# A two-layer gated cross-attention kernel: the place of the q_r products among the transposes

## The chip, the core and the metric

The kernel runs on one core of one Trainium2 chip. Its engines have queues of their own: TensorE (PE, matrix products and transposes), VectorE (DVE), ScalarE (ACT), GpSimd (POOL) and SyncE (SP, which here only issues DMAs). The metric is device time in microseconds, and lower is better.

## The reference

`x` has four batch rows of 512 tokens with 512 features; `ctx_512` is a context of 4 x 512 x 128. Two layers follow each other, each a gated mixing with the context and a gated feed-forward part:

```python
x = x + tanh(g_xattn[0]) * L0_xattn(ctx_512, layernorm(x), ...)   # top-k adjacency, 4 x 512 x 512
x = x + tanh(g_ffn[0])   * L0_ffn(layernorm(x), ...)              # Hadamard, 8-bit activations, ternary weights
x = x + tanh(g_xattn[1]) * L1_xattn(layernorm(x), ctx_512, ...)   # 16 heads, below
x = x + tanh(g_ffn[1])   * L1_ffn(layernorm(x), ...)              # 8-bit activations, ternary weights
```

The change lies in the third line. Cut to what matters, that attention is:

```python
q_hk  = (hidden_q @ Wq.T)                                 # 16 heads of 128
q_big = einsum('bshk,hkq->bshq', q_hk, w_kc_q)            # 384 per head
q_big = q_big * cos_q + rotate_half(q_big) * sin_q
kv_r  = kv_c * cos_k + rotate_half(kv_c) * sin_k
q_r   = einsum('bshq,hqr->bhsr', q_big, W_qr)             # 64 per head
k_r   = einsum('bld,hdr->bhlr', kv_r, W_kr)
attn  = softmax(einsum('bhsr,bhlr->bhsl', q_r, k_r))
ctx_c = einsum('bhsl,bld->bhsd', attn, kv_r)
out   = (ctx_c through w_kc_kv and Wo, summed over the heads)
```

## The kernel before

The attention of the second layer is the spine of the program. `attention` (L860) walks over 32 pairs of heads, eight for each batch row, in four steps `j` for the four token tiles of 128. A pair is an object of class `Pair` (L737). While the scores of the current pair `cur` are worked on, the queries of the next pair `nxt` are made:

- `scores(j)` (L798): the scores of both heads for token tile j into PSUM (`pss`, L806 and L809), their negated row maximum on VectorE (`nm`, L814), the exponential with its sum on ScalarE (`pp`, L817), and the scaling by 1/sum on ScalarE (L820).
- `head(i)` (L744): the query of one head of the next pair (`pqh`, L747), copied to `qh` by ScalarE.
- `rope(i)` (L755): two products with `wc` (`pb`, L762), then on VectorE a product with the cosine (`ro`, L770) and one or two with the sine (`rs`, L772 or L775), and on GpSimd their sum, back into `ro` (L776). `rope(2)`, called in step 3, makes the last two of the six `ro` tiles.
- `turn(j)` (L823): for each head four transposes of the probabilities of token tile j into one PSUM tile (`ppt`, L828), and ScalarE's copy to `pT` (L829). These PSUM tiles come from the pool `pst`, which has two.
- `rotated()` (L779): the load of the next `kr` (L783), then q_r of both heads of the next pair in one PSUM tile (`pr`): three steps, each of one product for the upper half of the partitions (L733) and one for the lower (L735), over the six `ro` tiles. The last step needs the two tiles of `rope(2)`. ScalarE copies `pr` to `qr` (L793).
- `attended()` (L831): eight products of `pT` with the context (`pc`, L836), copied to `cxo` by ScalarE (L841). `added()` (L844): eight products with the folded output weights (`po`, L848), and on VectorE the addition to x (L853).

`pr`, `pss`, `pqh`, `pb`, `pc` and `po` share the four PSUM tiles of the pool `ps`; `kr`, `qr` and `wr` have one buffer each, `ro` has seven, `pT` two.

Behind the spine runs background work, drawn step by step from generators at the `yield` of each j: for batch rows 1 to 3 first the adjacency of the first layer (20 rounds of top-k on VectorE, `m` L436 and `work` L441, given a low priority with `high_priority(offset=-FILL)`), then its feed-forward part (`feed0`); while the last batch row is in the attention, the weights of the last feed-forward part and that part itself (`feed1`) for the earlier rows. Row 0 goes through the first layer before the attention starts, and row 3 through the last feed-forward part after it ended.

The order on each engine isn't the order of the text. A scheduler in the compiler goes through the instructions with priorities that follow the text, and takes an instruction of lower priority when, by its own estimate, the one ahead of it isn't ready. The text's order is thus a preference; each engine's resulting queue is fixed when the program is built.

Of the kernel before, what the change touches and what calls it, by code (L numbers as in the profile page):

```python
# [17 lines left out]
NT = S // P  # L18
# [15 lines left out]
def flamingo_kernel(  # L34
# [661 lines left out]
    def hidden_T(b):  # L696
        mv, r = ln_stats([xs[b, j] for j in range(NT)], f"q{b}")
        t = hp.tile([P, NC, S], F32, tag="hT", name=f"hT_{b}", bufs=1)
        for j in range(NT):
            n = wp.tile([P, D], F32, tag="pp", name=f"nq_{b}_{j}", bufs=7)  # L700
            ln_tile(n, xs[b, j], j, mv, r)
            pt = tr_ps(f"phT_{b}_{j}")
            for c in range(NC):
                nc.tensor.transpose(pt[:, c, :], n[:, c * P : (c + 1) * P], ident)
            nc.scalar.copy(t[:, :, j * P : (j + 1) * P], pt)
        hT[b] = t
# [15 lines left out]
    def out_weights(b, g):  # L722

        oms = []
        for h in (2 * g, 2 * g + 1):
            om = hp.tile([P, D], F32, tag="om", name=f"om_{b}_{h}")
            nc.sync.dma_start(om, om_d[h])
            oms.append(om)
        return oms
# [125 lines left out]
    def begin(b, g):  # L855
        p = Pair(b, g)
        p.wqs, p.wc, p.wr = query_weights(b, g)
        return p

    def attention(first):  # L860


        order = [(b, g) for b in range(B) for g in range(NG)]
        cur = first
        for at, (b, g) in enumerate(order):
            nxt = begin(*order[at + 1]) if at + 1 < len(order) else None
            cur.oms = out_weights(b, g)
            fresh = nxt is not None and nxt.b != b
            for j in range(NT):
                cur.scores(j)  # L870
                if nxt:
                    if j == 0:
                        if fresh:
                            hidden_T(nxt.b)
                        nxt.head(0)
                    elif j == 1:
                        nxt.rope(0)
                        nxt.head(1)
                    elif j == 2:
                        nxt.rope(1)  # L880
                    else:
                        nxt.rope(2)
                if j > 1:
                    cur.turn(j - 2)
                yield b, g
            if nxt:
                nxt.rotated()
            cur.turn(NT - 2)
            cur.turn(NT - 1)
            cur.attended()  # L890
            cur.added()
            if g == NG - 1 and b < B - 1:
                for j in range(NT):
                    d = dram.tile([P, D], F32, tag=f"xd{b}_{j}", name=f"xd_{b}_{j}")
                    nc.sync.dma_start(d, xs[b, j])
                    spilled[b, j] = d
            cur = nxt
# [67 lines left out]
    for _ in attention(first):  # L965
        done += 1
        while job < len(jobs):
            gen, cost, until = jobs[job]
            start = jobs[job - 1][2] if job else 0
            want = cost * (done - start) / (until - start)  # L970
            ended = False
            while spent < want or done >= until:
                if f"g{B - 2}" in reached:

                    break
                try:
                    spent += next(gen)
                except StopIteration:
                    ended = True
                    break  # L980
            if not ended:
                break
            if done < until:

                jobs[job] = (iter(()), 0.0, until)
                break
            job, spent = job + 1, 0.0
# [127 lines left out]
```

## Time and profile before

| | |
|---|---|
| median of 3 runs | 2082.72 us (2080.54 to 2085.15) |
| the profiled execution | 2086.76 us, of which the profile's span is 2085.0 us |
| TensorE clock granted, mean | 0.972 of full |
| up to 285 us: first layer of row 0 and the preparation | TensorE busy 172.2 of 285 us |
| 285 to 1930 us: the attention with its background | TensorE busy 1556.2 of 1645 us |
| 1930 to 2085 us: the last pair and the last feed-forward | TensorE busy 135.8 of 155 us |
| q_r products (L733 and L735) | 192 matrix passes each, median 592 ns, the two halves side by side |
| transposes (L828) | 1024 passes, 272 to 475 ns each, overlapping one another |
| rotary addition (L776) | 192 on GpSimd, 1271 ns at the median |
| copies of pT (L829), of qr (L793) | 256 and 32 on ScalarE, 590 and 587 ns |

An instruction group of the profile gives the line, the engine, the operation, output and inputs by their names in the program, the count and the mean length. Lengths of matrix passes overlap, so a run of them is best read from one start to the next. "Idle before" is the time in which the engine stood still just ahead of an instruction, and the arrow names what ended it. In a table of windows each row has the stretch, its length, then busy time and count for TensorE, weight loads, VectorE, ScalarE and GpSimd, the granted clock, the DMA share and GB/s.

### The profile page before, as it was taken

The numbers are of one execution on the slowest core, as the hardware profiler recorded it, in microseconds if no ns is written. First come the engines' busy times: TensorE is split into PE (matmuls) and PEld (weight loads), VectorE is DVE, ScalarE is ACT, GpSimd is POOL, SyncE is SP. The second block draws the span as 40 slices with busy tenths as digits, with TensorE's granted clock in tenths as the row PEclk, the third lists the DMA queues.
The fourth block names the chain that finished last, engine by engine and source line by source line (L and its number), as shares of the span: only waits on it lengthen the run. The fifth ranks groups of instructions, "written<-read, shape, count | busy, mean of one in ns | idle before, by whom it ended". The sixth has DMA issues, their size and how long they took to land.

```text
span 2085.0 us, 21677 instructions
## 1 busy us (share of the span) xinstructions
PE 1864.1 (89%) x7274; PEld 876.8 (42%) x7274; DVE 1589.9 (76%) x3233; ACT 1182.9 (57%) x1982; POOL 331.0 (16%) x316
## 2 busy tenths in 40 slices
PE   1269889999999999999989999999889999999898
PEld 0135433444544444444544444445443444444444
DVE  6997689996675999967668999676645745856775
ACT  6936634354744554455455553554799565567554
POOL 3011121122101121131011211310111200111000
PEclk9779989999999999999999999999999999999999
DMA  7442211110100211111002111110656111111000
GB/s 268 149 141 107 83 37 48 44 46 27 38 20 27 86 50 41 47 32 33 25 27 87 49 47 38 37 33 20 224 185 225 55 31 46 57 32 46 11 16 26
DMA packets 62175, 137.66 MB, mean 66 GB/s; under 512 B 7152, under 2 KB 14704, under 8 KB 58992
## 3 DMA queue, kind: packets, MB, share of 16 engines
q1 hardware_dynamic: 56592, 120.35, 18.2%
q0 software_dynamic: 4320, 14.16, 1.8%
q10 hardware_dynamic: 1152, 1.77, 0.2%
q8 instruction: 58, 0.95, 0.2%
q14 instruction: 53, 0.43, 0.1%
HBM read 116.33 MB, written 19.92 MB: 65 GB/s over the span
## 4 chain that ended last, share of the span: by engine, by line
PE 52%; DVE 29%; ACT 11%; DMA 3%; POOL 2%; issue 2%; ACTq 0%; SPq 0%; POOLq 0%; DVEq 0%
PE pc L836 8%; PE po L848 6%; PE pqh L747 6%; DVE work L441 4%; DVE m L436 4%; DVE nm L814 4%; PE pb L762 3%; PE pzh_f L550 3%; PE pr L733 3%; PE pss L806 3%; PE pu_f L291 2%; DVE rs L775 2%; PE pg_f L291 2%; DVE ro L770 2%; PE pu_g L291 2%; PE pd_g L386 2%
## 5 line engine op out<-in xcount | busy, mean ns | idle before, releaser
L776 POOL TENSOR_TENSOR ro<-ro,rs 128x512 f32<-128x512 f32 x192 | 250.3, 1306 | 1333.8 <-DVE rs L772 722.5
L817 ACT ACTIVATE pp<-pss,nm 128x512 f32<-128x512 f32 x256 | 175.1, 688 | 224.6 <-DVE nm L814 223.9
L747 PE MATMUL pqh<-hT,wq 128*128 128x512 f32 x512 | 240.6, 609 | 4.0 <-ACT pp L817 2.5
L836 PE MATMUL pc<-pT,kv 128*128 128x512 f32 x512 | 233.5, 598 | 6.0 <-ACT pT L829 6.0
L848 PE MATMUL po<-om,cxo 128*128 128x512 f32 x512 | 231.4, 596 | 0.5 <-ACT cxo L841 0.5
L814 DVE TENSOR_REDUCE nm<-pss 128x1 f32<-128x512 f32 x256 | 167.6, 680 | 70.4 <-PE pss L809 70.0
L762 PE MATMUL pb<-qh,wc 128*128 128x512 f32 x384 | 191.7, 617 | 7.4 <-DVE ro L770 3.8
L436 DVE MAX8 m<-work 128x8 f32<-128x512 f32 x304 | 197.6, 680 | 0.5
L441 DVE MATCH_REPLACE8 work<-m,work 128x512 f32<-128x512 f32 x288 | 192.9, 675 | 0.1
L820 ACT ACTIVATE pp<-pp,rsm 128x512 f32<-128x512 f32 x256 | 179.2, 725 | 17.7 <-DVE rsm L819 17.1
L829 ACT COPY pT<-ppt 128x512 f32<-128x512 f32 x256 | 143.2, 590 | 36.9 <-PE ppt L828 36.8
L828 PE MATMUL ppt<-ident,pp 128*128 128x128 f32 x1024 | 149.3, 280 | 11.4 <-ACT pT L829 9.2
L853 DVE SCALAR_TENSOR_TENSOR x<-po,gt,x 128x512 f32<-128x512 f32 x128 | 94.5, 743 | 82.6 <-PE po L848 81.5
L828 PEld LDWEIGHTS ppt<-ident,pp 128*128 128x128 f32 x1024 | 116.4, 142 | 92.5 <-issue 45.6
L806 PE MATMUL pss<-kr,qr 64*128 64x512 f32 x256 | 145.6, 649 | 9.0 <-ACT pp L817 7.5
L747 PEld LDWEIGHTS pqh<-hT,wq 128*128 128x128 f32 x512 | 93.7, 193 | 126.9 <-issue 93.1
L809 PE MATMUL pss<-kr,qr 64*128 64x512 f32 x256 | 145.5, 649 | 0.0
L848 PEld LDWEIGHTS po<-om,cxo 128*128 128x128 f32 x512 | 94.4, 190 | 113.7 <-issue 95.7
L770 DVE TENSOR_TENSOR ro<-pb,cos_q 128x512 f32<-128x512 f32 x192 | 130.4, 679 | 15.1 <-PE pb L762 14.3
L836 PEld LDWEIGHTS pc<-pT,kv 128*128 128x128 f32 x512 | 93.0, 191 | 102.8 <-issue 90.5
L733 PE MATMUL pr<-ro,wr 128*64 128x512 f32 x192 | 100.6, 625 | 29.5 <-POOL ro L776 28.3
L841 ACT COPY cxo<-pc 128x512 f32<-128x512 f32 x64 | 37.5, 586 | 135.3 <-PE pc L836 135.1
(266 smaller groups left out, 3132.8 us busy)
## 6 DMA issues: line engine op xcount, KB each, us to landing
wq<-in_wqh SPq DMA_DIRECT2D x64, 256.0 KB, 2.7
om<-omd SPq DMA_DIRECT2D x64, 256.0 KB, 2.7
wc<-in_wkcq SPq DMA_DIRECT2D x32, 384.0 KB, 3.1
krd<-krs POOLq DMA_DIRECT2D x32, 256.0 KB, 2.5
kr<-krd SPq DMA_DIRECT2D x32, 256.0 KB, 2.7
sa_w1v<-in_gvT SPq DMA_DIRECT2D x8, 1024.0 KB, 5.6
sb_w1v<-in_gvT SPq DMA_DIRECT2D x8, 1024.0 KB, 5.5
wr<-in_wqr SPq DMA_DIRECT2D x32, 192.0 KB, 2.4
```

The source lines that it names most:

```text
L436: nc.vector.max(m8[j], cur[j])
L441: nc.vector.match_replace(works[j], m8[j], cur[j], GONE)
L747: nc.tensor.matmul(pq, self.wqs[i][:, c, :], hT[self.b][:, c, :], start=(c == 0), stop=(c == NC - 1),)
L762: nc.tensor.matmul(pb, self.wc[:, at : at + P], self.qhs[i if i < 2 else o], start=True, stop=True)
L776: nc.gpsimd.tensor_tensor(ro, ro, rs, ALU.add)
L806: nc.tensor.matmul(*args, start=True, stop=True)
L814: nc.vector.tensor_reduce(nm, pss[i], AX.X, ALU.max, negate=True)
L817: nc.scalar.activation(pp, pss[i], AF.Exp, bias=nm, accum_out=sm)
L820: nc.scalar.activation(pp, pp, AF.Copy, scale=rs)
L828: nc.tensor.transpose(pt[:, l, :], pp[:, l * P : (l + 1) * P], ident)
L836: nc.tensor.matmul(pc, kv[self.b][:, l, :], self.pT[i][:, l, :], start=(l == 0), stop=(l == NT - 1),)
L848: nc.tensor.matmul(po, self.cxo[i][:, j * P : (j + 1) * P], self.oms[i], start=(i == 0), stop=(i == 1),)
```

## The change

In `attention`, behind the four steps of a pair, three calls change places: both remaining `turn` calls of the current pair (token tiles 2 and 3) come first in the text, and `rotated()` of the next pair follows them, still ahead of `attended()`.

```diff
                 if j > 1:
                     cur.turn(j - 2)
                 yield b, g
+            cur.turn(NT - 2)
+            cur.turn(NT - 1)
             if nxt:
                 nxt.rotated()
-            cur.turn(NT - 2)
-            cur.turn(NT - 1)
             cur.attended()
             cur.added()
```

Nothing else is edited. The first pair's `rotated()`, called ahead of the attention, and the last pair, which has no next, stay as they are. The priorities of the moved instructions change, and with them the queues that the scheduler builds on TensorE, VectorE and ScalarE, also for background work around them.

## The prediction

> **What bounds the kernel now.** I read the page first, then busy time by window, then who waits for whom on TensorE, then the timeline of single ends of a pair of heads (below: a tail; the tails are numbered 1 to 31, tail n ending where the products with the context of the n-th pair start).
>
> ```profile
> PE 1864.1 (89%) x7274; PEld 876.8 (42%) x7274; DVE 1589.9 (76%) x3233; ACT 1182.9 (57%) x1982; POOL 331.0 (16%) x316
> PE   1269889999999999999989999999889999999898
> ```
>
> The page's first two parts: TensorE is busy 89% of the span, and after the first eighth there are few gaps. So only gaps of TensorE are to be had, and the longest kind that repeats is the one that the change touches:
>
> ```profile
> PE pr L733 <- POOL ro L776: 28.3, 25, 2.9
> PE ppt L828 <- ACT pT L829: 9.2, 29, 1.6
> PE pc L836 <- ACT pT L829: 6.0, 16, 1.9
> ```
>
> The waits of TensorE (total us, times, longest): the products that make q_r (pr) wait for GpSimd's last rotary addition, the transposes (ppt) for ScalarE to empty their PSUM banks, the products with the context (pc) for the last of these copies. 43.5 us together; this is the ceiling. One tail, on TensorE and on ScalarE (start, length, what, and in brackets idle time and releaser):
>
> ```profile
> 354.67 0.59 PE L733 MATMUL pr<-ro,wr 128*64 128x512 f32 x1
> ...
> 355.20 1.09 PE L828 MATMUL ppt<-ident,pp 128*128 128x128 f32 x8
> 356.53 0.44 PE L828 MATMUL ppt<-ident,pp 128*128 128x128 f32 x2 [0.24 <-ACT pT L829]
> 358.05 0.64 PE L733 MATMUL pr<-ro,wr 128*64 128x512 f32 x1 [1.08 <-POOL ro L776]
> ...
> 359.06 0.87 PE L828 MATMUL ppt<-ident,pp 128*128 128x128 f32 x6
> 360.32 0.70 PE L836 MATMUL pc<-pT,kv 128*128 128x512 f32 x1 [0.39 <-ACT pT L829]
> ```
>
> ```profile
> 359.20 0.59 ACT L793 COPY qr<-pr 128x512 f32<-128x512 f32 x1 [2.23 <-PE pr L735]
> 359.68 1.08 ACT L829 COPY pT<-ppt 128x512 f32<-128x512 f32 x2
> ```
>
> The scheduler has already pulled ten of the sixteen transposes in front of the last products of q_r. Six are still behind them, and the copies of these are behind the copy of q_r on ScalarE, which sits 2.23 us waiting. Then the windows from pc to pc (TensorE, weights, VectorE, ScalarE, GpSimd), two with top-k work and two later ones:
>
> ```profile
> 319.40:360.30 40.90, 38.56 (x120) 16.39 (x120) 40.49 (x89) 17.90 (x38) 7.62 (x6) 1.00 0.16 47
> 743.20:784.00 40.80, 38.93 (x122) 16.48 (x120) 40.58 (x90) 18.27 (x39) 7.64 (x6) 1.00 0.17 47
> 1546.10:1588.40 42.30, 38.71 (x124) 16.57 (x123) 19.60 (x40) 39.97 (x54) 7.63 (x6) 1.00 0.78 275
> 1672.00:1742.70 70.70, 69.00 (x284) 30.81 (x283) 43.81 (x71) 44.80 (x69) 7.59 (x6) 1.00 0.12 35
> ```
>
> In the first two VectorE is busy 40.5 of 40.9 us: there the pair lasts as long as VectorE's queue, whatever TensorE does. In the third ScalarE binds (40.0 of 42.3), in the fourth TensorE (69.0 of 70.7). So a gap of TensorE is worth its length in some tails only.
>
> **What the skill says.** The Trainium skill, "TensorE: Matmul & The Clock Gate" (row "Engine queue depth" of the table at the top): weight loads can be pulled ahead, ScalarE's, VectorE's and GpSimd's queues are strictly first in, first out; and its Part 3, "What overlaps and what doesn't", says that matmuls start and end in program order. The trace agrees: the transposes of 359.06 sat behind the waiting product of 358.05, and two copies behind the waiting copy of q_r. So what stands behind what decides here. "Perfetto Trace Analysis", "Identifying Performance Opportunities", warns that matmul busy time overstates how near TensorE is to its best; I use starts and gaps, not busy sums. "GPSIMD Engine Reference", "Key points": GpSimd shares its SBUF interface with VectorE; the rotary addition takes 1.27 us at the median and 2.24 at most, so the arrival of the last operand isn't sharp.
>
> **The change, part by part.** No instruction and no DMA is added or removed. On SyncE the load of kr keeps its place among the others, so it and the loads behind it cost nothing: kr is needed by the next scores, behind eight products pc and eight po (6.9 us each in the chain). On TensorE the orders of both programs, set side by side, show what moves. Before, a tail mostly goes: eight transposes, two steps of q_r, twelve transposes or so, last step of q_r, the rest, pc. After: one step, four transposes, one step, eight, last step, four or none, pc.
>
> (a) Transposes moved in front of the last step. Their arrival of operands is fixed by VectorE and GpSimd, so each fills part of the wait. Counting those behind the last step, before minus after, over the 20 tails that show the wait and keep their surroundings: 66. A transpose is 1.04 us / 8 = 0.13 us. 66 x 0.13 = 8.6 us of the 28.3.
> (b) Copies of the transposes now stand in front of the copy of q_r on ScalarE, so pc doesn't wait: of the 6.0 us, 3.0 in the tails of (d), about 2 in the others.
> (c) The wait of a transpose for its bank (0.24 us each) goes where no wait for q_r follows, as a step of q_r now stands in the gap: six tails, 0.24 us and the 0.19 us ahead of pc, 0.43 us each.
> (Cost) Two steps in a row took 353.33 to 355.20, 1.87 us; one alone 358.05 to 359.06, 1.01. So each split costs 2 x 1.01 - 1.87 = 0.15 us. Ahead of a wait it is hidden; I count five where it isn't: 0.75 us. Without that cover all 26 splits would cost 3.9 us.
>
> (d) VectorE-bound tails (1 to 4, 9 to 12, 17 to 20): 42 of the 66 transposes, 5.5 us, and 3.0 us of (b), 8.5 us at TensorE. But VectorE's idle time over the eleven windows is 8.6 us in all (0.4, 1.8, 0.4; 0.4, 0.2, 1.9, 0.5 twice), and its queue holds the same work. What it can give: bits of that idle time, and top-k steps that the new order puts off to the next stretch (at most three of 0.7 us in the first batch row, one in the others). Bounds 0 and 8.5; I take 3.0.
> (e) The other tails: 24 transposes 3.1 us; six times 0.43 = 2.6; tail 23, where pc waits 1.86 us behind ScalarE's weight work and one step of q_r (1.01) now stands in that gap, 1.0; tail 7, 0.5. 7.2 - 0.75 = 6.4 us.
>
> (d) and (e) make 9.4 us. TensorE has 89 us of idle time between 285 and 1930 us (span minus busy in those windows), 41 of it in these waits; the other 48 are waits for VectorE, ScalarE and POOL that grow when TensorE comes sooner and their producers don't. I take two thirds, 6 us. For the profiled execution, 2086.76 us (span 2085.0, 1.8 around it), this gives 2080.8; that execution lies 4.0 above the median of the runs, 2082.72, so the forecast is 2076.7.
>
> Unknown: in the second batch row the queued feed-forward work near 480 to 570 us is reshuffled (about 6 us of VectorE's work comes one pair sooner, and four GpSimd steps of 0.74 us stand ahead of the last rotary additions in one tail). From its rows it could cost 3 us (4 x 0.74) or gain as much, since TensorE idles 4.2 us in the window from 441.7 to 493.2; I take 0 and keep 3 both ways.
>
> **Rivals.**
> 1. Hidden anyway: VectorE and ScalarE bind more than I allow, (d) gives 0 and half of (e) is taken by the next wait: -3 us, 2079.7; with the reshuffle at a loss, 2082. For it: 98 to 99% in the windows above. Against: VectorE is idle a third of the time in the windows of (e).
> 2. More: all of (d) comes, as VectorE's last 0.5 us per pair wait for po: -6.4 - 8.5 + 3 for later waits, about -12, 2070.8. For it: a wait of 0.47 us of VectorE for po at 369.30. Against: nothing leaves VectorE's queue.
> 3. Slower, through VectorE's queue: the new program puts the updates of x (L853) one top-k step (0.68 us) sooner in the VectorE-bound stretches, 24 of them. If TensorE isn't that much sooner there, VectorE waits for po with the top-k steps and the next row maxima (nm, L814) queued behind, and exponentials and TensorE wait for these. 18 of 24 x 0.68 = 12.2 us, minus 6.4: +6, 2088.6. It decides from some 16 such stalls. For it: x started 0.04 to 0.8 us after po ended in these tails, so there is no slack. Against: TensorE is to come 0.5 to 0.9 us sooner in the same tails, and a step pushed behind a wait doesn't lengthen the queue.
>
> **How the numbers follow.** Forecast 48%, rival 1 25%, rival 2 7%, rival 3 20%. About 0.2%, 4.2 us, is what a measurement of this kernel can tell from no change: faster is below 2078.5, slower above 2086.9. The forecast's own range is 2073 to 2080; part of it (a tenth of the whole) is within 0.2%, and rival 1 lies almost wholly there; a little of rival 3 ends there too. Faster 0.47, same 0.33, slower 0.20. The range reaches from 2070 to 2087: it leaves out most of rival 3 and the lower end of rival 2.
>
> **What would show it.** Waits of pc for pT near 2 us; waits of pr for POOL near 20; ScalarE's copy of q_r with no copies of transposes behind it; the windows with top-k still 40 to 41 us long and VectorE at 40; windows with feed-forward work 0.3 to 1 us shorter. I am wrong if VectorE's wait for po in the top-k windows grows by several us (rival 3), if these windows shrink by more than 0.7 us (rival 2), or if the gap ahead of pr grows by what the others lose.

## The result, and the profile after

The changed kernel takes 2069.74 us at the median of six runs (2068.03 to 2072.59). The kernel before took 2083.93 us over six runs, so the ratio is 0.9931, interval 0.9914 to 0.9948: 14.2 us less, where 6 were forecast. Six later runs of the same kernel gave 2070.15 us, 0.9921 (0.9908 to 0.9934) of the kernel before beside them.

The profiled execution of the changed kernel has a span of 2067.4 us, 17.6 less than that of before (2085.0). That difference is 3.4 us larger than that of the medians: the profiled execution of before lay 2.8 us above its median, this one 0.5 below. First the busy times, from the page:

```profile
PE 1864.0 (90%) x7274; PEld 875.2 (42%) x7274; DVE 1589.6 (77%) x3233; ACT 1179.9 (57%) x1980; POOL 331.3 (16%) x316
```

TensorE was busy 1864.1 us before. So the work is the same, and all 17.6 us are idle time of TensorE that is gone. The waits of TensorE (total us, times, longest), and the page's group of the products with the context, whose last number is the idle time ahead of them:

```profile
PE pr L733 <- POOL ro L776: 18.4, 19, 2.9
...
PE ppt L828 <- ACT pT L829: 7.3, 21, 0.7
```

```profile
L836 PE MATMUL pc<-pT,kv 128*128 128x512 f32 x512 | 233.8, 598 | 0.2 <-ACT pT L829 0.2
```

The wait for the rotary addition went from 28.3 to 18.4 us, that of the transposes from 9.2 to 7.3, and that of the products with the context from 6.0 to 0.2: 17.6 of the 43.5 us (by chance the same figure as the difference of the spans, since other waits moved both ways). The same tail as before the change, on TensorE and then on ScalarE (start, length, what, in brackets idle time and releaser):

```profile
355.04 1.09 PE L828 MATMUL ppt<-ident,pp 128*128 128x128 f32 x8
357.15 0.64 PE L733 MATMUL pr<-ro,wr 128*64 128x512 f32 x1 [1.02 <-POOL ro L776]
...
358.16 0.66 PE L828 MATMUL ppt<-ident,pp 128*128 128x128 f32 x4
358.65 1.02 PE L836 MATMUL pc<-pT,kv 128*128 128x512 f32 x2
```

```profile
355.73 1.07 ACT L829 COPY pT<-ppt 128x512 f32<-128x512 f32 x2 [0.79 <-PE ppt L828]
358.30 0.59 ACT L793 COPY qr<-pr 128x512 f32<-128x512 f32 x1 [1.50 <-PE pr L735]
358.86 0.59 ACT L829 COPY pT<-ppt 128x512 f32<-128x512 f32 x1
```

Four transposes instead of six stand behind the last step of q_r, and only one copy of transposes behind the copy of q_r. The wait of that step itself is nearly as long (1.02 us for 1.08); the tail is shorter because more of its other work was done by then. Now the windows that answer to the four shown before (length, then busy time and count of TensorE, weights, VectorE, ScalarE, GpSimd; clock, DMA share, GB/s):

```profile
318.80:358.70 39.90, 38.26 (x123) 16.18 (x122) 39.54 (x89) 17.92 (x38) 7.62 (x6) 1.00 0.16 48
734.70:774.80 40.10, 38.92 (x123) 16.49 (x122) 39.91 (x89) 18.06 (x38) 7.63 (x6) 1.00 0.17 48
1530.20:1572.70 42.50, 39.34 (x122) 16.89 (x122) 18.64 (x38) 41.97 (x55) 7.63 (x6) 1.00 0.85 294
1653.60:1720.60 67.00, 65.00 (x266) 28.91 (x265) 38.91 (x64) 43.56 (x67) 7.59 (x6) 1.00 0.14 40
```

VectorE is still full in the first two, 39.5 of 39.9 us. But the windows went from 40.9 and 40.8 to 39.9 and 40.1, and VectorE has 1.0 and 0.7 us less to do in them. The fourth is 3.7 us shorter with 4.0 us less of TensorE's work: that work moved, and the window behind it is 4.2 us longer. So a window with feed-forward work says little by itself. All windows of both executions, added up by kind:

| windows (from pc to pc) | change in length | of TensorE's idle time |
|---|---|---|
| 0 to the first pc (about 319 us) | -0.7 | -2.8 |
| eleven with top-k work | -6.9 | -8.9 |
| the three at the end of the top-k work (441.7, 866.0, 1287.2 before) | -1.9 | +1.3 |
| those with feed-forward work, rows 0 to 2 | -6.3 | -5.8 |
| last batch row and the end | -1.7 | -1.2 |

Where did the work of VectorE go that left the eleven windows? The three windows that follow them, before and then after:

```profile
441.70:493.20 51.50, 47.33 (x186) 23.24 (x185) 42.85 (x97) 24.36 (x47) 18.86 (x22) 0.97 0.13 39
866.00:917.10 51.10, 47.38 (x185) 23.51 (x186) 41.77 (x96) 24.21 (x47) 18.86 (x22) 0.97 0.15 41
1287.20:1336.70 49.50, 45.79 (x185) 22.71 (x186) 41.75 (x96) 23.57 (x46) 18.86 (x22) 1.00 0.14 39
```

```profile
438.40:489.70 51.30, 47.05 (x194) 23.57 (x192) 45.09 (x108) 24.18 (x47) 19.46 (x22) 1.00 0.15 43
855.30:904.70 49.40, 45.07 (x179) 21.93 (x177) 43.00 (x98) 23.32 (x45) 18.86 (x22) 1.00 0.14 39
1272.50:1321.90 49.40, 45.07 (x179) 21.93 (x177) 42.98 (x98) 23.31 (x45) 18.86 (x22) 1.00 0.13 39
```

Here VectorE does 2.2, 1.2 and 1.2 us more (42.85 to 45.09, and so on), and none of these windows is longer: VectorE had 8.7, 9.3 and 7.7 us idle in them. In the eleven windows VectorE's idle time fell from 8.6 to 5.4 us, so 3.2 us of the 6.9 are idle time filled. Its busy time fell by the other 3.7 us. Five top-k steps fewer start there (three in the first batch row, one in each of the next two), which at their mean lengths is 2.8 us; together with four from other windows they stand in the three windows shown, whose top-k steps went from 28 to 37. The last 0.9 us isn't accounted for.

### The profile page after: what moved, and what is told of

Same layout as the page of the kernel before. It is cut to its first block, busy times and chain, and to the rows that moved or that the text cites. A ratio compares the mean times of both kernels' runs of the same rounds, so it can differ in the third digit from the quotient of the medians.

```text
span 2067.4 us, 21667 instructions
## 1 busy us (share of the span) xinstructions
PE 1864.0 (90%) x7274; PEld 875.2 (42%) x7274; DVE 1589.6 (77%) x3233; ACT 1179.9 (57%) x1980; POOL 331.3 (16%) x316
## 4 chain that ended last, share of the span: by engine, by line
PE 49%; DVE 33%; ACT 11%; DMA 3%; issue 2%; POOL 1%; ACTq 0%; SPq 0%; POOLq 0%; DVEq 0%
PE pc L836 7%; PE po L848 6%; PE pqh L747 6%; DVE work L441 5%; DVE m L436 5%; DVE nm L814 4%; DVE ro L770 3%; PE pzh_f L550 3%; DVE rs L775 3%; PE pu_f L291 2%; PE pss L806 2%; PE pu_g L291 2%; PE pg_f L291 2%; PE pd_f L386 2%; PE pr L733 2%; PE pb L762 2%
## 5 line engine op out<-in xcount | busy, mean ns | idle before, releaser
L817 ACT ACTIVATE pp<-pss,nm 128x512 f32<-128x512 f32 x256 | 175.1, 688 | 224.8 <-DVE nm L814 223.5
L441 DVE MATCH_REPLACE8 work<-m,work 128x512 f32<-128x512 f32 x288 | 193.0, 675 | 0.1
L733 PE MATMUL pr<-ro,wr 128*64 128x512 f32 x192 | 102.0, 620 | 20.4 <-POOL ro L776 18.4
```

Of the source, the lines that this page charges most:

```text
L441: nc.vector.match_replace(works[j], m8[j], cur[j], GONE)
```

## The experiments

Three theories stood after the result. Local: the gain is made in the tails, by transposes that fill the wait for q_r's last operands (the prediction's a) and by copies no longer behind the copy of q_r (its b). Reshuffle: much of the sum comes from background work that the scheduler places otherwise. And for the tails with top-k work, that a full VectorE takes part of the gain. Times of the kernel before that stand beside a run are from the same chip, in turn with it. The expectations of the first four runs name theories by letters: A is that each group of tails makes its own gain and that the two add up; the other letters are rivals to it, in which they don't or one group has it all.

### One group of tails at a time

The new order in the tails with top-k work alone, and in all others alone:

```diff
+            late = b < B - 1 and g < 4      # second kernel: not (b < B - 1 and g < 4)
+            if nxt and not late:
+                nxt.rotated()
             cur.turn(NT - 2)
             cur.turn(NT - 1)
-            if nxt:
+            if nxt and late:
                 nxt.rotated()
```

> The new order only in the tails that lie in the stretches with top-k work (pairs 0 to 3 of batch rows 0 to 2, tails 1-4, 9-12, 17-20); the old order in the others. Theory A (the gain is a sum of tails, each worth what its own window lost): the windows ending in these tails lost 0.4 to 1.3 us each in the changed kernel, 7.6 us in all, so -7 to -9 us against before, about half of the change's 14; the windows with top-k work come out as in the changed kernel (39.6 to 40.3 us). Theory B (what I said beforehand: VectorE binds there and only 3 us are to be had, the rest of the 14 comes from the other tails): -2 to -4 us. Theory C (the large part is an accident of the reshuffled feed-forward work in the fifth to seventh pair of the second batch row, which follows from the earlier end of the adjacency): -7 to -9 plus the 5 us of that window, -12 to -14.

> The complement: the new order in all other tails, the old one in the stretches with top-k work. Theory A (sum of tails): -5 to -8 us, so that this and its complement add up to the change's 14. Theory B (VectorE binds in the top-k stretches): -10 to -12. Theory C (the reshuffle after the first top-k stretch makes the big part): -1 to -3, as the reshuffle is not triggered here.

The first took 2074.9 us against 2083.34, 0.9956 (0.9943 to 0.997): -8.4. The second took 2078.1, 0.9975 (0.996 to 0.9989): -5.2. Together 13.6, against 14.2 for the whole, each with an interval of about 3 us either way. In the traces the eleven top-k windows are 6.9 us shorter in the first and unchanged (0.4 us longer) in the second. So for these tails A holds, and they, which the prediction priced lowest since VectorE is full there, gave about half. For the others it isn't shown. The totals add up, but the windows don't: the two from 493.2 to 649.1, 4.7 us shorter with the whole change, are 0.9 us shorter in the first kernel, which has the old order there, and 1.6 us longer in the second, which has the new one.

### The copy of q_r late, the products in their old place

`rotated()` keeps its old place but leaves its copy to a call behind both turns:

```diff
-            self.qr = wp.tile([P, S], F32, tag="qr", name=f"qr_{u}", bufs=1)
-            nc.scalar.copy(self.qr, pr)
+            self.pr = pr
...
             cur.turn(NT - 1)
+            if nxt:
+                with tc.issue_after(cur.last.ins):   # the last copy of transposes
+                    nxt.kept()                       # the copy of pr to qr
```

> The products of q_r stay in their old place on TensorE; only ScalarE's copy of q_r is put behind the last two copies of transposes. If the wait of pc for these copies (6.0 us in all) is what the change removed, most of that comes back here: pc's wait for pT falls to 2 us or less, -3 to -5 us. If the transposes that moved in front of the last q_r step are the larger part, this kernel gets no more than a third of the change's gain, and the windows with top-k work shrink by 0.3 us at most. If ScalarE's order is irrelevant: within 2 us of before.

2071.59 us, 0.9943 (0.993 to 0.9956): -11.75, far more than expected. Read by the total alone, this says that ScalarE's queue is four fifths of the gain. The windows say otherwise. The eleven with top-k work lose only 1.7 us in sum. Most of the rest is in pairs of windows with feed-forward work; one pair, before and then in this kernel:

```profile
917.10:989.10 72.00, 70.98 (x306) 34.68 (x304) 49.40 (x76) 36.13 (x66) 6.03 (x4) 1.00 0.10 28
989.10:1070.30 81.20, 76.52 (x365) 41.42 (x365) 59.29 (x85) 39.53 (x76) 10.99 (x8) 0.96 0.09 27
```

```profile
913.00:991.60 78.60, 77.10 (x349) 38.91 (x349) 53.75 (x78) 45.06 (x77) 7.63 (x6) 1.00 0.09 28
991.60:1059.30 67.70, 65.64 (x312) 34.86 (x312) 51.63 (x75) 35.79 (x68) 9.52 (x6) 1.00 0.11 29
```

153.2 us became 146.3, with 43 matrix passes more in the first window and 53 fewer in the second. Background work fell into other places. Is that a gain of the late copy, or of this one program? Two kernels and the bare runs below answer.

### The late copy joined with the new order

First the changed kernel with the copy of q_r held behind the last copy of transposes; then the late copy in all tails, with the new order in the top-k tails and the old order in all others, which would take the best windows of both.

> The changed order, and ScalarE's copy of q_r issued only behind the last copy of the transposes (as in the run with the late copy). Local theory: ScalarE's queue is already in this order in nearly all tails of the changed kernel, so within 2 us of it, about 2070 us. Reshuffle theory: anywhere between 2062 and 2078 us, with the windows of top-k work as in the changed kernel (39.6 to 41.1 us) and the whole difference in windows with feed-forward work.

> The changed order in the tails with top-k work (first four pairs of batch rows 0 to 2), the old order with the late copy of q_r in the others. If the gains found in the windows of the two runs add up (7 us in the windows with top-k work, 12 us in those with feed-forward work): about 2065 us, better than the changed kernel. If the gain of the late copy in the feed-forward windows was a matter of how the background fell in that one program: about 2072 us or more.

2073.34 us, 0.9951 (0.9937 to 0.9965), and 2080.61 us, 0.9984 (0.9973 to 0.9994). The first lies 3.6 us above the changed kernel, more than the 2 us expected if only the tails counted. The second kernel keeps the late copy in the very tails where it seemed to gain, and the gain is gone. Its pair of windows:

```profile
909.90:982.00 72.10, 71.04 (x307) 34.75 (x305) 49.49 (x76) 37.14 (x68) 6.06 (x4) 1.00 0.11 31
982.00:1062.60 80.60, 75.80 (x364) 40.90 (x364) 59.20 (x85) 38.91 (x75) 11.04 (x8) 0.98 0.09 27
```

72.1 and 80.6 us, as before the change. So what the late copy brought in these windows was the way in which the background happened to fall.

### How much the fall of the background is worth

One number of the planner, in both kernels; nothing of the tails is edited:

```diff
-    jobs = [(before(b), 230.0, b * per - NT) for b in range(1, B)]
+    jobs = [(before(b), 236.0, b * per - NT) for b in range(1, B)]
```

> The kernel before with one number changed: the planned cost of a row's background 236 instead of 230, so that each of its steps comes a little later. Nothing in the tails is edited. Local theory: within 3 us of before. Reshuffle theory: a change of 3 to 10 us either way, most of it in the windows with feed-forward work.

> The changed kernel with the same number, 236 instead of 230. Local theory: 11 to 17 us below the run before it. Reshuffle theory: the difference to the run before it lies anywhere from +2 to -20 us, and not near -14; the windows with top-k work are 7 us shorter in sum in any case.

The kernel before became 2080.02 us against 2085.58, 0.9972 (0.996 to 0.9984), 5.6 us less with the tails untouched. The changed one took 2068.36, 0.9921 (0.9906 to 0.9936), 11.7 below the former. The same window of the spine in four programs: before, before shifted, changed, changed shifted.

```profile
571.50:649.00 77.50, 71.80 (x322) 37.76 (x320) 53.21 (x75) 35.84 (x68) 8.53 (x6) 0.93 0.10 27
```

```profile
570.80:643.50 72.70, 69.70 (x322) 35.93 (x321) 55.75 (x79) 35.86 (x69) 8.51 (x6) 0.98 0.10 29
```

```profile
568.50:640.80 72.30, 69.55 (x314) 36.59 (x313) 49.41 (x69) 35.97 (x67) 8.52 (x6) 0.95 0.10 27
```

```profile
569.80:636.30 66.50, 64.70 (x311) 34.41 (x309) 51.46 (x75) 35.62 (x67) 7.72 (x6) 1.00 0.10 29
```

77.5, 72.7, 72.3 and 66.5 us: the changed kernel's largest single gain is the 5.2 us in this window, and the shift alone brings 4.8. A second one, 1.7 us in the window from 866.0, comes with the shift as well (51.1 to 49.5). The clock has a share in both. An estimate from its column in the four lines above: it takes up to (1 - 0.93) x 77.5 = 5.4 us, then 1.5, 3.6 and nothing. The window from 866.0 had clock 0.97 before and 1.00 in the others (0.03 x 51.1 = 1.5 us), while its like from 1287.2, at 1.00 throughout, kept its length (49.5 and 49.4). The top-k windows, all at clock 1.00, don't depend on the shift: 6.9 us shorter without it, 6.5 with it.

### No background at all

In both kernels, and then in the one with the late copy, the top-k adjacency and first feed-forward part of batch rows 1 to 3 are left out, and x is loaded as it is:

```diff
     def before(b):
-        yield from adjacency(b)
-        yield from feed0(b, w0)
+        for k in range(80):
+            if k == 40:
+                for j in range(NT):
+                    t = xp.tile([P, D], F32, tag="x", name=f"x{b}_{j}")
+                    nc.sync.dma_start(t, x[(b * NT + j) * P : (b * NT + j + 1) * P, :])
+                    xs[b, j] = t
+            yield 2.7
```

> The kernel before, with the background work of batch rows 1 to 3 (their top-k adjacency and first feed-forward part) left out, so that the pairs of the first 23 tails run alone. It is the yardstick for the next run. Both theories: clearly shorter than before, since 390 matrix passes per row and all top-k work are gone; the waits of pr for GpSimd stay, some 1 us in each tail.

> The changed kernel with the same background left out. Local theory (the gain is made in the tails themselves, about 0.6 us a tail, by transposes in the wait for q_r's last operands and by copies no longer behind the copy of q_r): 8 to 17 us less than the run before it. Reshuffle theory (about half of the 14.2 us comes from feed-forward and top-k steps that the scheduler places otherwise): 4 to 8 us less, as only the tails' own gain is left.

> No background in batch rows 1 to 3, the old order of the products, and ScalarE's copy of q_r issued behind the last copy of the transposes (the edit of the late-copy run). If the copies on ScalarE are what counts, as the late-copy run's total suggests: its standard window is 38.9 us or less, four fifths of the way from 40.0 to 38.7, and the time about 1784 us. If the transposes in the wait for q_r count: the wait of pr stays near 40 us in sum, the window 39.5 to 39.8 us, and the time 1800 us or more.

1815.14 us (1813.37 to 1816.09) and 1776.02 us (1775.83 to 1777.5): the same change is worth 39 us here, more than either theory expected. With the late copy alone it is 1810.43 us (1805.88 to 1813.91), on a chip where the kernel before takes 4.4 us less too. One tail, before and changed:

```profile
696.09 0.64 PE L733 MATMUL pr<-ro,wr 128*64 128x512 f32 x1 [1.39 <-POOL ro L776]
...
697.10 0.98 PE L828 MATMUL ppt<-ident,pp 128*128 128x128 f32 x7
698.37 1.13 PE L836 MATMUL pc<-pT,kv 128*128 128x512 f32 x2 [0.28 <-ACT pT L829]
```

```profile
685.29 1.09 PE L828 MATMUL ppt<-ident,pp 128*128 128x128 f32 x8
686.67 0.64 PE L733 MATMUL pr<-ro,wr 128*64 128x512 f32 x1 [0.29 <-POOL ro L776]
...
687.68 1.13 PE L836 MATMUL pc<-pT,kv 128*128 128x512 f32 x2
```

Seven transposes, 0.98 us, moved into the wait, which went from 1.39 to 0.29 us, and pc no longer waits 0.28. 1.10 + 0.28 is 1.38; the windows that end there show it, before, changed, and with the late copy:

```profile
658.40:698.40 40.00, 38.09 (x121) 16.39 (x121) 17.93 (x34) 17.57 (x38) 7.58 (x6) 1.00 0.18 47
698.40:739.50 41.10, 39.47 (x120) 17.02 (x120) 17.93 (x34) 17.58 (x37) 7.59 (x6) 0.96 0.16 48
```

```profile
649.00:687.70 38.70, 38.03 (x123) 16.21 (x121) 17.93 (x34) 17.90 (x38) 7.59 (x6) 1.00 0.18 50
```

```profile
656.20:696.20 40.00, 38.11 (x121) 16.41 (x121) 17.93 (x34) 17.61 (x38) 7.58 (x6) 1.00 0.16 48
```

40.0, 38.7 and 40.0 us at full clock, and so in each of the eighteen windows of this kind: at clock 1.00 the change is worth 1.17 to 1.36 us in them, mostly 1.26. That is the tail's own worth where nothing else is full. The late copy is worth 0.05. With no background this settles it between (a) and (b): the transposes count, the order on ScalarE by itself hardly does. In the whole kernel the late copy took 1.7 us off the eleven top-k windows; how much of that is its own isn't known. The waits of TensorE for the rotary addition agree: 40.9 us in all in the first run, 16.4 in the second, 40.7 with the late copy.

The eighteen windows lose 30.4 us together (the spans of the two profiles differ by 36.1), of which 18 x 1.26 = 22.7 is the tails' worth. The other 7.7 us go with the clock: six of the eighteen have a mean clock of 0.95 to 0.98 before the change, like the second line of the first fence (0.96, 1.1 us longer), and none has after it.

### How much the full VectorE takes

In the top-k windows of the whole kernel the change is worth 6.9 / 11 = 0.63 us each, half of 1.26. Not all of that is VectorE's doing: the first top-k windows of batch rows 1 and 2 (from 702.3 and 1123.5) gain only 0.07 and 0.48 us with no background either. The other nine gave 7.2 us, 0.80 each. The first try left out every second replacement pass (`work`, L441) in batch rows 1 to 3, by a condition on `r`, the second three of four whole rounds there:

```diff
             for r in range(rounds):
+                if not alone[0] and r % 4:
+                    yield 2.7
+                    continue
                 with tc.high_priority(offset=-FILL):
```

> The kernel before, with every second replacement pass of the top-k search (L441) left out in batch rows 1 to 3, so that VectorE has some 7 to 9 us less to do in each of the windows with top-k work and no longer fills them. It is the yardstick for the next run. Both theories: these windows near 40 us, as in the run with no background at all, with VectorE idle for 6 us or more in each.

> The changed kernel with the same passes left out. If a full VectorE is what halved the gain in the windows with top-k work (0.63 us a window there, 1.26 us with no background): these eleven windows are now 1.1 to 1.4 us shorter each than in the run before it, 12 to 15 us in sum. If something else halves it (TensorE filled by other work, later waits): 0.5 to 0.8 us each, 6 to 9 us in sum.

> The kernel before, with three of four top-k rounds left out in batch rows 1 to 3, so that VectorE is idle for 5 us or more in the windows with top-k work. It is the yardstick for the next run; these windows near 40 to 41 us.

> The changed kernel with the same rounds left out. If a full VectorE halves the gain in the windows with top-k work: those of these windows in which VectorE is idle for 5 us or more and TensorE has no feed-forward work are 1.1 to 1.4 us shorter than in the run before it. If something else does: 0.4 to 0.8 us.

The first pair, 2064.91 and 2056.48 us, tells nothing: in eight of the eleven windows VectorE was idle for only 0.2 to 4.1 us, not the 6 that were wanted, and the eleven lost 9.3 us in sum, between the two forecasts. The second pair took 2059.42 and 2050.87 us. Two windows of each, before and changed:

```profile
735.20:775.10 39.90, 38.16 (x126) 16.66 (x124) 23.00 (x45) 18.07 (x39) 7.59 (x6) 1.00 0.16 49
775.10:815.20 40.10, 38.33 (x125) 16.79 (x124) 20.69 (x38) 17.68 (x38) 7.59 (x6) 1.00 0.17 49
```

```profile
731.50:770.20 38.70, 38.04 (x122) 16.23 (x120) 20.48 (x42) 17.66 (x37) 7.59 (x6) 1.00 0.17 50
770.20:809.00 38.80, 38.34 (x125) 16.50 (x123) 20.35 (x37) 17.66 (x37) 7.60 (x6) 1.00 0.17 49
```

With VectorE at 18 to 23 us, five windows of this kind lost 1.22, 1.23, 1.32, 1.23 and 1.32 us, as with no background. In the whole kernel the same five lost 1.28, 0.77, 1.05, 0.78 and 1.05 us, 0.99 at the mean. The third of them there, before and changed:

```profile
784.00:825.20 41.20, 38.66 (x124) 16.83 (x124) 39.31 (x87) 22.35 (x44) 7.61 (x6) 1.00 0.17 47
```

```profile
774.80:815.00 40.20, 38.82 (x125) 16.44 (x123) 38.74 (x85) 22.74 (x44) 7.63 (x6) 1.00 0.17 48
```

So where the two can be compared, a full or nearly full VectorE takes about a fifth of a tail's worth, not two thirds or all. In the other six windows VectorE was still full, or the clock or feed-forward work differs; that it takes half there isn't shown.

### Farther in the same direction

q_r's last step held behind the last transpose, first in all tails, then without those that have feed-forward work of rows 1 to 3; and q_r as a whole behind the products with the context. The changed kernel ran beside the first two.

```diff
-        def rotated(self):
+        def rotated(self, behind=None):
...
-                halves(...)
+                with ExitStack() as held:
+                    if behind is not None and o == 2:
+                        held.enter_context(tc.issue_after(behind.ins))   # last transpose of cur
+                    halves(...)
```

```diff
             cur.turn(NT - 1)
+            cur.attended()
             if nxt:
                 nxt.rotated()
-            cur.attended()
             cur.added()
```

> The changed kernel once more, beside the two runs that follow. Both theories: about 2070 us.

> The changed kernel with q_r's last step held behind the last transpose in every tail, where the changed kernel still leaves up to four transposes behind that step in some. If the transposes in the wait for q_r's last operands are what counts: the wait of pr for GpSimd falls from 18.4 us to 10 us or less, windows with top-k work lose up to 0.5 us more where four transposes stood behind, and the time is 2 to 6 us under the changed kernel, give or take the 5 us by which the background falls otherwise. If they don't count: no gain, or a loss where the last step now waits for ScalarE to empty a bank.

> The same, but only in the tails of the first four pairs of batch rows 0 to 2 and in the last batch row. In tails with feed-forward work of rows 1 to 3, TensorE has other work to fill the wait, so nothing is lost there: within 4 us of the run before it, and 2 to 6 us under the changed kernel if the transposes count.

> The products of q_r one step further back, behind all eight products with the context, ahead of those with the output weights. The wait of pr for GpSimd, still 18.4 us in the changed kernel, goes almost wholly; the tails lose 1 us each where it was left. If TensorE's gaps in the tails count at full value: -22 to -28 us against before. If VectorE binds in the top-k stretches (windows at 39.6 to 40.3 us now), these gain nothing more, and it is -15 to -20. If q_r then comes too late for the next scores (its copy stands behind both copies of the context on ScalarE), pss waits for qr and it is slower than the changed kernel.

The changed kernel gave 2070.15 us, the next two 2071.71 (0.9936, 0.9924 to 0.9948) and 2072.94 (0.9942, 0.9929 to 0.9954). They were to be 2 to 6 us faster than the changed kernel. The wait fell nearly as far as was expected, and two top-k windows of the first of them:

```profile
PE pr L733 <- POOL ro L776: 12.4, 15, 2.9
```

```profile
359.90:399.50 39.60, 38.49 (x124) 16.47 (x122) 38.10 (x83) 22.64 (x43) 7.64 (x6) 1.00 0.17 48
735.70:775.70 40.00, 39.08 (x122) 16.44 (x120) 39.81 (x91) 18.05 (x37) 7.64 (x6) 1.00 0.16 48
```

12.4 us for 18.4, and the windows stay at 39.6 and 40.0 us (39.5 and 40.1 in the changed kernel). The second has VectorE at 39.8 of 40.0 us, so there the next bound is reached. In the first VectorE is idle for 1.5 us, and why it gains nothing is open. I found no version that is faster than the changed kernel by more than its runs scatter.

Behind the products with the context the time is 2128.35 us, 1.0211 (1.0196 to 1.0226), 45 us more. The waits of TensorE in it, and one window with top-k work that took 40.8 us before:

```profile
PE ppt L828 <- ACT pT L829: 33.1, 52, 2.8
...
PE ppt L828 <- ACT pp L820: 12.7, 6, 3.6
```

```profile
826.60:879.00 52.40, 43.79 (x138) 19.71 (x137) 49.19 (x110) 21.36 (x41) 11.00 (x11) 0.91 0.13 37
```

The wait for the rotary addition is down to 4.3 us, but the transposes now wait in a row for ScalarE's copies, 33.1 us for 9.2, with no step of q_r between them; and the window shown and the one behind it grow by 12 and 20 us, partly with feed-forward work that stood in later windows before (one of these is 26 us shorter). The case feared beforehand, scores that wait for q_r, isn't seen: TensorE's weight loads wait for it for 1.6 us in all, 2.0 before. How the 45 us divide wasn't tried.

## Why the prediction was wrong in its size

Its direction, its place and its mechanism (a) hold. Point by point:

- The wait for the rotary addition was to fall to about 20 us: 18.4. That of pc to about 2: 0.2. The 8.5 us of TensorE in the tails of (d) are about right: TensorE's idle time in the eleven windows fell by 8.9 us, 6.9 by shorter windows and 2.0 by other work that came in.
- **The step that failed is (d): "I take 3.0".** The windows gave 6.9 us, and the kernel with these tails alone 8.4. The text named both sources, idle time of VectorE and top-k steps put off, and mis-sized their sum. VectorE filled 3.2 us of its idle time, and all five steps that the text had counted (three, one and one) were put off, in the 3.7 us by which its busy time fell; their room was in sight, 8.7, 9.3 and 7.7 us of VectorE's idle time in the windows behind. The text took a queue that is 99% busy as a bound on the window's length. It was a bound only for the work that must be done there, and the top-k steps need not be. Of the 8.2 us by which the forecast fell short, 3.9 are this term; with 6.9 in its place (d) and (e) would have made 13.3 us ahead of the last step.
- "I take two thirds" for later waits, 3.4 us off: in the eleven windows nothing was taken, as the 6.9 us are net of such waits. For the other tails the runs don't tell, since the fall of the background moved the same windows by as much.
- (b), worth some 5 us by itself, isn't a term of its own. The copies come early because their transposes do; ScalarE's order alone is worth 0.05 us a tail with no background, and 1.7 us at most in the eleven windows.
- (e), 6.4 us: the other tails alone took 5.2 us off. But some 7 of the profile's 17.6 us stand in two windows that gained nearly as much by the shift of the planner (5.2 and 1.7 us), with the clock in part. Without these the windows behind the first pc that are not among the eleven gave about 3. That this sum came out near the measured 5.2 was luck.
- "I take 0 and keep 3 both ways" for the reshuffle was too narrow: a shift that touches no tail moved the kernel before by 5.6 us, and one window ranged over 11 us in four programs.
- The second rival, "all of (d) comes", was nearest in its time (2070.8) and in the size of (d) (6.9 of 8.5 us), but not in its cause: VectorE's waits for po in the top-k windows were 1.5 us in all before and 0.5 after. Its own sign, windows with top-k work shorter by more than 0.7 us, appeared in six of eleven. The third rival, a slower kernel, had the order of VectorE's queue right, but the stalls that it needed didn't come: the same 0.5 us. The first, that the gain is hidden anyway, falls with the 6.9 us.

## What to carry to other kernels

An engine that is busy all the time bounds a stretch only by the work that can't leave it: look for low-priority steps in its queue, and for idle time of the same engine in the next stretch, before you call a gain at another engine hidden. Where a scheduler places background work, a harmless shift of that work tells how far a total can move for reasons that aren't the edit's; judge a small edit by the windows that the background doesn't reach, or with the background left out. A total alone would here have put most of the gain on ScalarE's queue, whose order is worth 0.05 us a tail with no background.

## What the runs showed that was not expected

A short gap of TensorE went with a lower clock. With the background left out and a gap of 1.4 us in each tail, six of eighteen like windows had clock 0.95 to 0.98 and were about 1.0 to 1.7 us longer; with the gap at 0.3 us, none. In the run with the late copy, whose gap is as long, it was six again, but not the same six. The clock record of the first of these runs shows what the means hide, here at the end of one tail:

```profile
442.60:446.00 3.40, 1.77 (x13) 1.19 (x13) 1.67 (x3) 1.20 (x3) 2.25 (x2) 1.00 0.01 4
446.00:449.40 3.40, 3.40 (x12) 1.76 (x9) 0.00 (x0) 1.36 (x3) 0.00 (x0) 0.51 0.18 56
```

Each lower mean is one stretch of 3.41 us at half clock, and these stretches start whole multiples of 3.41 us apart (446.04, 487.00, 736.17 us). I cut TensorE's time between 326 and 1276 us of this run at the same steps: of the 13 steps with 1.62 us or more of idle time, 9 are followed by half clock, of the 257 with less, none. The gap of 1.39 us and the wait of 0.24 us ahead of it make 1.63 us, so it takes both in one step, which not every tail has. Nobody varied the idle time alone, so this is what went together and not a cause that was shown.

q_r behind the context made ScalarE load activation tables 133 times instead of 107, at 1.283 us each, 33 us more of its time: 59 for 46 times at the exponentials (L817) and 42 for 31 at the background's L296, which alternate more often. The Trainium skill, "ScalarE activation tables: per-element evaluation and per-set limits", "What a function is on this engine", gives the same 1283 ns for a change of set; the changed kernel has 105 loads, so they are worth 2.6 us of ScalarE's time in its gain at most. Whether the 33 us lay on the path in the slow kernel wasn't tried.
